# A convolution-attention kernel: six-block slots replaced by eight-block batches, with PSUM and the exponentials as rings

## The chip, the cores and the metric

The kernel runs on one core of a Trainium2 chip. The metric is the device time of one execution in microseconds (us); the time before is the median of three runs. The trace was taken in one further execution by the hardware profiler, and its own time is given beside its span below.

Five engines matter. TensorE (PE in the profile; PEld is its loading of weights) multiplies matrices into PSUM, which has eight banks of 512 float32 a partition. ScalarE (ACT) does the exponentials and most copies out of PSUM, VectorE (DVE) the convolution and most of the elementwise work. GpSimd (POOL) and SyncE (SP) issue transfers for the most part.

## The reference

The input has 4 images of 384 channels and 48 x 48 pixels, so 2304 tokens an image. There are 8 heads of 48 channels.

```python
x_flat = x.reshape(B, C, N).transpose(0, 2, 1)
local = lax.conv_general_dilated(x, conv_w, (1, 1), 'SAME', feature_group_count=C)   # 7 x 7, depthwise
local = local * inv[None, :, None, None] + (bn_beta - bn_mean * inv)[None, :, None, None]
local_flat = local.reshape(B, C, N).transpose(0, 2, 1)
x_norm = _layernorm(x_flat, ln_gamma, ln_beta)
qkv = x_norm @ qkv_w.T + qkv_b
q, k, v = ...                                              # (B, heads, tokens, 48) each
q = q + _layernorm(local_flat, ln_gamma, ln_beta) by heads
attn = softmax(einsum('bhnd,bhmd->bhnm', q, k) * 48 ** -0.5)
out = einsum('bhnm,bhmd->bhnd', attn, v) by tokens @ proj_w.T + proj_b
return (x_flat + out) as an image
```

## The kernel before, in words

**Tiling.** Everything is float32. The queries of an image are cut into five groups of whole rows: 8, 10, 10, 10 and 10 rows of 48 pixels, so 384 columns in the first group and 480 in the others ("narrow" and "wide" in the prediction). Over four images that is 20 groups, t = 0 to 19; t // 5 is the image and t % 5 the group in it. The keys of an image are cut into 18 blocks of 128 tokens, and the 8 heads into 4 pairs (p). A group therefore has 4 x 18 = 72 pieces of work ("blocks"), one for each head pair and key block.

**One block.** `score` (line 1143) makes the scores of 128 keys against the group's queries for both heads of a pair: three passes (the queries and keys are split into a high and a low part, tile `qs` and tile `ks`), each a pair of matmuls, one on each 64-row half of TensorE, so six matmuls into a tile `r` of two PSUM banks, one bank a head. ScalarE then writes the exponentials of both banks in one instruction of 960 (or 768) columns to a tile `pt` in SBUF (line 1151). `weigh` (line 1158) multiplies values by those exponentials: one pair of matmuls, one for each head, each writing one 64-row half of a PSUM bank `o`. In the trace and in the order below a matmul is shown in parts where the hardware counts it in parts: a block has 6 score instructions and 4 value instructions there, or 3 and 2 pairs. The value products of the blocks add up in PSUM. The softmax's denominators come out of the same product, from a column of ones beside the values.

**The slot.** A group runs in `NSLOT` = 12 slots of `BATCH` = 6 blocks, three slots to a head pair. A slot first issues all six scores with their exponentials (`score_batch`), then all six value products (`weigh_batch`), and then `sums_out`: ScalarE copies the sums of the slot from PSUM, at the first slot of a head pair straight to the output tile `ao` or `aot` (line 1045), else to a tile `part_o` (line 1035, named `o` in the profile), which VectorE adds to the output tile in the next slot (`sums_add`, line 1054). PSUM is a pool of four tiles of two banks, taken in turn by scores, sums and everything else (`two_banks`). The exponentials have four buffers.

**What runs beside it.** TensorE, VectorE, ScalarE and SyncE execute their instructions in the order in which the program is written; nothing is reordered. Beside the attention of a group the other engines prepare the next one:

- VectorE computes the 7 x 7 convolution of the next group's rows, one tap of one third of the channels at a time (line 367, tile `acc`). How many taps stand at which place is planned when the program is built: `spare` says for each half of each slot how much of VectorE's time is free, `due` when the taps of each group must be done, and `plan` spreads them. `convolve` issues the planned number. The first taps of a group are ScalarE's (line 330, queued through `soon`).
- The sums are normalized over the 384 channels (`Norm`). In the first image (t = 0 to 3, "early" in the code) the mean is made by TensorE (line 616), kept in SBUF by ScalarE (line 609), subtracted by VectorE, squared by ScalarE (`square_jobs`, line 588), and the root is three activations: logarithm, exponential, square (`root`, lines 652 to 654). VectorE then refines the root (`newton`, from line 666), scales the sums and adds the query projection (line 992, tile `xn`). In the later images the means go through DRAM, so that few elements are left for the root.
- A group's queries are split for each head pair: the high part is a ScalarE cast (`high_queries`, line 1006), the low part a VectorE subtraction (`low_queries`, line 1011), followed by six small transfers that fill the rest of the 128 partitions (lines 1016 and 1018), half of them on SyncE and half on another queue.
- Keys lie in DRAM (`wide`), and stacks of six blocks are loaded by GpSimd's queue two slots before they are needed (`load_keys`, line 801).
- Between two images the projections of the next image run for 140 us on TensorE (line 729). The change does not touch their matmuls.

The order of all this is written out by hand in the loop over slots at the end of the program: after the scores of a slot comes a list of conditions on the slot number, then the first half's taps (`convolve("slot", t, s, 0)`), `sums_add`, more conditions, the value products (with the queued `jobs`, the squares, ahead of them), the second half's taps, and again a list of conditions.

## Time and profile before

| | before |
|---|---|
| median of three runs | 2724.02 us (2722.55 to 2724.08) |
| span of the profiled execution | 2720.3 us |
| TensorE busy | 2707.9 us, 100% of the span |
| VectorE busy | 2314.8 us, 85% |
| ScalarE busy | 1671.1 us, 61% |
| GpSimd busy | 592.7 us, 22% |
| mean granted TensorE clock | 1.000 |
| DMA | 370.46 MB, mean 136 GB/s |

The profiled execution is one execution, of which the profile gives the span, 2720.3 us from the first to the last instruction; its time as the three runs are timed is not recorded apart. The span lies 3.7 us under the median.

How to read the rows of the prediction: in a group of instructions stand line, engine, operation, output and inputs with their shapes and the count, then the busy time in us, the mean time of one in ns, and the idle time of the engine just before these instructions with what ended most of it. In the timeline stand the start in us from the span's beginning, the length in us of a run of like instructions, the engine and what they are with their count (x36), and in brackets, where the engine waited before it, how long and for whom. A timeline cut to a window shows of a run only the instructions that start in the window, so the same run appears with smaller counts, and the difference of two starts divided by the difference of the counts gives the pace. Two matmuls on the two halves of TensorE make a pair. In the row that begins with 246.90:357.40, these are the ends of the stretch; then come its length, the busy us and count of TensorE, its weight loads, VectorE, ScalarE and GpSimd, the granted clock, and the DMA's busy share and GB/s.

### The profile page before, as it was taken

The numbers are of one execution on the slowest core, as the hardware profiler recorded it, in microseconds if no ns is written. First come the engines' busy times: TensorE is split into PE (matmuls) and PEld (weight loads), VectorE is DVE, ScalarE is ACT, GpSimd is POOL, SyncE is SP. The second block draws the span as 40 slices with busy tenths as digits, with TensorE's granted clock in tenths as the row PEclk, the third lists the DMA queues.
The fourth block names the chain that finished last, engine by engine and source line by source line (L and its number), as shares of the span: only waits on it lengthen the run. The fifth ranks groups of instructions, "written<-read, shape, count | busy, mean of one in ns | idle before, by whom it ended". The sixth has DMA issues, their size and how long they took to land.

```text
span 2720.3 us, 46072 instructions
## 1 busy us (share of the span) xinstructions
PE 2707.9 (100%) x16468; PEld 1532.5 (56%) x16468; DVE 2314.8 (85%) x4042; ACT 1671.1 (61%) x2318; POOL 592.7 (22%) x1061
## 2 busy tenths in 40 slices
PE   9999999999999999999999999999999999999999
PEld 6565555555566555555555655555555665555555
DVE  8999999989899999989889999889889898986212
ACT  4366767777326777777622767767752377676762
POOL 3541111112452111011165111111225501110110
PEclk9999999999999999999999999999999999999999
DMA  8454544545455545455455554544635544444442
GB/s 176 91 160 124 140 125 127 134 129 160 129 139 164 145 118 142 124 143 138 122 152 144 154 146 120 139 132 129 167 96 160 151 141 123 147 128 132 139 151 68
DMA packets 160129, 370.46 MB, mean 136 GB/s; under 512 B 58273, under 2 KB 107234, under 8 KB 159890
## 3 DMA queue, kind: packets, MB, share of 16 engines
q0 software_dynamic: 70688, 277.77, 36.0%
q1 hardware_dynamic: 83456, 79.29, 12.9%
q10 hardware_dynamic: 5746, 10.36, 1.1%
q8 instruction: 132, 2.16, 0.3%
q14 instruction: 107, 0.88, 0.1%
HBM read 258.14 MB, written 64.14 MB: 118 GB/s over the span
## 4 chain that ended last, share of the span: by engine, by line
PE 93%; DVE 5%; DMA 1%; ACT 0%; issue 0%; SPq 0%; DVEq 0%; ACTq 0%
PE o L1158 41%; PE r L1143 33%; PE r L729 18%; DVE acc L367 4%; DMA xn<-in_x_dram 1%; DMA staged<-in_qkv_wT_dram 0%; PE r L616 0%; DVE k L839 0%; DMA slab<-in_x_dram 0%; DVE sq L593 0%; DVE ao L1054 0%; SPq L116 0%; PE r L634 0%; DVE xn L644 0%; DVE sq L594 0%
## 5 line engine op out<-in xcount | busy, mean ns | idle before, releaser
L367 DVE SCALAR_TENSOR_TENSOR acc<-slab,vec,acc 128x470 f32<-128x470 f32 (+10 forms) x2832 | 1656.9, 656 | 2.0 <-ACT acc L330 2.0
L1151 ACT ACTIVATE pt<-r 128x960 f32<-128x960 f32 (+1 forms) x1440 | 1248.4, 943 | 244.1 <-PE o L1158 150.4
L1158 PE MATMUL o<-pt,v 128*64 128x480 f32 (+1 forms) x5760 | 1166.1, 554 | 0.4 <-ACT pt L1151 0.4
L1143 PE MATMUL r<-qs,ks 64*128 64x480 f32 (+1 forms) x8640 | 965.8, 373 | 1.6 <-ACT xn L853 0.7
L1143 PEld LDWEIGHTS r<-qs,ks 64*128 64x128 f32 x8640 | 783.6, 184 | 265.6 <-issue 168.2
L1158 PEld LDWEIGHTS o<-pt,v 128*64 128x64 f32 x5760 | 392.9, 137 | 659.2 <-issue 566.8
L801 POOL DMA_DIRECT2D ks<-wide x220 | 159.9, 727 | 1375.7 <-PE r L1143 1333.1
L729 PE MATMUL r<-xn,w_qk 128*128 128x384 f32 x864 | 284.2, 486 | 0.0
L1035 ACT COPY o<-o 113x480 f32<-113x480 f32 (+1 forms) x160 | 87.0, 544 | 275.6 <-PE o L1158 275.4
L729 PEld LDWEIGHTS r<-xn,w_qk 128*128 128x128 f32 x864 | 164.0, 190 | 114.7 <-issue 0.7
L823 ACT COPY v<-r 128x384 f32<-128x384 f32 x72 | 32.0, 480 | 190.3 <-PE r L729 190.3
L729 PE MATMUL r<-w_v,xn 128*128 128x384 f32 x432 | 145.0, 488 | 0.9 <-ACT sq L654 0.5
L1054 DVE TENSOR_TENSOR ao<-ao,o 113x480 f32<-113x480 f32 (+1 forms) x120 | 75.8, 631 | 75.2 <-ACT o L1035 75.2
L729 PEld LDWEIGHTS r<-w_v,xn 128*128 128x128 f32 x432 | 81.4, 190 | 59.9 <-issue 2.9
L786 POOL DMA_DIRECT2D wide<-k x144 | 71.7, 500 | 115.5 <-ACT k L836 79.4
L1011 DVE TENSOR_TENSOR qs<-xn,qs 128x480 fp32r<-128x480 f32 (+1 forms) x60 | 38.0, 633 | 59.1 <-ACT qs L1006 59.1
L729 PE MATMUL r<-af,w_o 128*128 128x384 f32 (+1 forms) x270 | 85.2, 470 | 0.0
L1045 ACT COPY ao<-o 113x480 f32<-113x480 f32 (+1 forms) x60 | 32.6, 544 | 74.3 <-PE o L1158 74.3
L1054 DVE TENSOR_TENSOR aot<-aot,o 113x480 f32<-113x480 f32 (+1 forms) x40 | 25.2, 631 | 58.5 <-ACT o L1035 58.5
L853 ACT ACTIVATE xn<-r,qkb 128x384 f32<-128x384 f32 x72 | 40.2, 577 | 55.1 <-PE r L729 53.8
L1124 DVE SCALAR_TENSOR_TENSOR xr<-r,pb,xr 128x384 f32<-128x384 f32 (+2 forms) x72 | 42.0, 611 | 36.8 <-PE r L729 28.1
L729 PEld LDWEIGHTS r<-af,w_o 128*128 128x128 f32 x270 | 51.3, 190 | 31.9
(154 smaller groups left out, 1338.8 us busy)
## 6 DMA issues: line engine op xcount, KB each, us to landing
ks<-wide POOLq DMA_DIRECT2D x220, 768.0 KB, 5.1
qs<-qs SPq DMA_DIRECT2D x346, 60.0 KB
slab<-in_x_dram POOLq DMA_DIRECT2D x22, 432.0 KB, 6.4
wide<-k POOLq DMA_DIRECT2D x96, 96.0 KB, 2.2
wide<-ks POOLq DMA_DIRECT2D x12, 768.0 KB, 5.1
xr<-in_x_dram POOLq DMA_DIRECT2D x16, 576.0 KB, 5.4
rb<-rden SPq DMA_DIRECT2D x32, 270.0 KB
held<-ao POOLq DMA_DIRECT2D x12, 720.0 KB, 4.1
```

Of the source, the lines that this page charges most:

```text
L367: nc.vector.scalar_tensor_tensor(dst, src, weight, dst, ALU.mult, ALU.add)
L729: nc.tensor.matmul(dst, lhsT=weights(c), rhs=src(c), start=c == 0, stop=c == CC - 1)
L786: nc.gpsimd.dma_start(out=last[16 * u : 16 * u + 16, 0], in_=k[r : r + 16, 0])
L801: queue.dma_start(out=place_keys(b, p, i), in_=wide[b, p][:, :, at])
L853: nc.scalar.activation(src[:, i, :], q[:, :G], AF.Identity, bias=qkb[:, 0, i : i + 1])
L1011: nc.vector.tensor_sub(qs[:, 1, :], query_of(t, p), qs[:, 0, :])
L1035: nc.scalar.copy(part[0 : 64 + HA], sums[0 : 64 + HA, 0, :n])
L1054: nc.vector.tensor_add(dst, dst, part[0 : 64 + HA])
L1124: nc.vector.scalar_tensor_tensor(xr[:, co, :], m, pb[:, co : co + 1], xr[:, co, :], ALU.add, ALU.add)
L1143: nc.tensor.matmul(r[:, j, :n], lhsT=ks[rows, w, at], rhs=qs[rows, m, :], start=i == 0, stop=i == 2,)
L1151: nc.scalar.activation(pt, r[:, :, :n], AF.Exp, scale=SCALE)
L1158: nc.tensor.matmul(sums[halves[j], 0, : columns_of(t)], lhsT=values[t // NA, kb // NB][:, first : first + 64], rhs=pt[:, j, :], start=i == ...
```

## The change

**Batches.** A group runs in 9 batches of 8 blocks instead of 12 slots of 6 (`BATCH`, `NBATCH`). 18 blocks of a head pair are not a multiple of 8, so some batches hold the end of one pair and the start of the next (in a group counted from 1: batches 3, 5 and 7); such a batch uses both banks of its sums' tile, one for each pair, and copies the first out inside the value products and the second behind them. Instead of 4 copies straight to the output and 8 partial sums there are 4 and 8 again (12 sums a group), and `part_o` has one buffer instead of two.

**Rings.** PSUM is one tile of eight banks, and `two_banks` deals out the next two of them in turn; before, a pool of four two-bank tiles did. The exponentials lie in one tile `pt` of nine halves (`2 * SPLIT + 1`, a half being 480 columns), taken in turn, two a block. As nine is odd, one block in nine has its two halves at the two ends of the tile; its exponential is two instructions of half the width (line 1167) instead of one (line 1171).

**Order in a batch.** The scores of all eight blocks are issued one after the other. The exponentials of blocks 1 to 4 and the first half of block 5's are issued with their scores. The second half of 5 and those of 6, 7 and 8 are queued (`exps`) and issued one each behind the value products of blocks 1, 2, 3 and 4, whose halves of the tile they take. In the prediction 5a and 5b are the two halves of the fifth.

**The steps beside it.** The conditions on the slot number are replaced by a table of steps (`steps_of`): each batch has four places, 0 in the middle of the scores (ahead of block 5), 1 behind them, 2 in the middle of the value products (behind block 4), 3 behind them. The convolution's taps are planned for these quarters (`spare`), with `AHEAD`, the point from which the next group's sums begin, at 24 instead of 18. The queued `jobs` are issued behind the first value product and the exponential that follows it, and the three activations of the root in groups t = 1 to 3 are one such job now. Keys are loaded by `next_keys`, as many stacks ahead as before.

The core of the diff, without the planner's numbers and the table's entries that keep their order:

```diff
-BATCH = 6
-NSLOT = 12
+BATCH = 8
+THIRD = 6
+SPLIT = 4
...
-AHEAD = 18
+AHEAD = 24
...
-    ps = ctx.enter_context(tc.tile_pool(name="ps", bufs=4, space=bass.MemoryType.PSUM))
+    ps = ctx.enter_context(tc.tile_pool(name="ps", bufs=1, space=bass.MemoryType.PSUM))
...
-    def two_banks(name="r"):
-        return ps.tile([P, 2, 512], F32, tag="r", name=name)
+    banks = ps.tile([P, 8, 512], F32, tag="banks", name="banks")
+    weights_of = big.tile([P, 2 * SPLIT + 1, GM], F32, tag="pt", name="pt")
+    n_banks = n_weights = 0
+
+    def two_banks():
+        nonlocal n_banks
+        i = n_banks % 8
+        n_banks += 2
+        return banks[:, i : i + 2, :]
...
-        pt = work.tile([P, 2, GM], F32, tag="pt", name="pt", bufs=4)[:, :, :n]
-        nc.scalar.activation(pt, r[:, :, :n], AF.Exp, scale=SCALE)
-        weighing.append((t, p, kb, pt))
...
+        n_halves = 2 * SPLIT + 1
+        first, second = n_weights % n_halves, (n_weights + 1) % n_halves
+        n_weights += 2
+        weighing.append((t, p, kb, (first, second)))
+
+        def exp_of(i, j):
+            nc.scalar.activation(weights_of[:, i, :n], r[:, j, :n], AF.Exp, scale=SCALE)
+
+        def exp_of_both():
+            if second:
+                nc.scalar.activation(
+                    weights_of[:, first : second + 1, :n], r[:, :, :n], AF.Exp, scale=SCALE
+                )
+            else:
+                exp_of(first, 0)
+                exp_of(second, 1)
+
+        if i < SPLIT:
+            exp_of_both()
+        elif i == SPLIT:
+            exp_of(first, 0)
+            exps.append(lambda: exp_of(second, 1))
+        else:
+            exps.append(exp_of_both)
...
-    def weigh_batch(t, s):
-        p, i = s // (KB // BATCH), s % (KB // BATCH)
-        while jobs:
-            jobs.popleft()()
-        while soon:
-            soon.popleft()()
-        sums = two_banks("o")
-        for n in range(BATCH):
-            weigh(n, sums)
-        ended.append((t, p, i, sums))
-        sums_out()
+    def score_batch(t, s, middle):
+        for i, (p, kb) in enumerate(blocks_of(s)):
+            if i == SPLIT:
+                middle()
+            score(t, p, kb, i)
+        return two_banks()
+
+    def weigh_batch(s, t, sums, middle):
+        blocks = blocks_of(s)
+        for n, (p, kb) in enumerate(blocks):
+            j = p - blocks[0][0]
+            start, stop = kb == 0 or n == 0, kb == KB - 1 or n == BATCH - 1
+            weigh(sums[:, j, :], start, stop)
+            if exps:
+                exps.popleft()()
+            if n == 0:
+                while jobs:
+                    jobs.popleft()()
+            if stop:
+                first = p * KB // BATCH
+                ended.append((t, p, s - first, kb == KB - 1, sums[:, j, :]))
+            if n == SPLIT - 1:
+                while soon:
+                    soon.popleft()()
+                middle()
+            if stop:
+                sums_out()
...
+            at(first, 3, lambda: norm.mean_of_sum())
+            at(first + 1, 0, lambda: norm.centre(), lambda: jobs.extend(norm.square_jobs()))
+            if t:
+                at(first + 1, 2, lambda: norm.sum_squares())
+                at(first + 1, 3, lambda: norm.mean_of_sum())
+                at(first + 2, 0, lambda: jobs.extend(norm.root_jobs()))
+                at(first + 2, 2, early_end)
+                at(first + 3, 0, high)
+                at(first + 3, 1, low)
...
+            sums = score_batch(t, s, lambda: step(0))
+            next_keys(b, g, s)
+            step(1)
+            weigh_batch(s, t, sums, lambda: step(2))
+            step(3)
```

How this moves instructions shows at three places. The first is TensorE at the head of the second group (t = 1, the first wide one), before. `qs_0` are its queries of the first head pair, `ks_0_0` to `ks_0_2` the three key stacks of that pair; a row of x36 is six blocks of scores, one of x12 their value products.

```order
L1143 MATMUL r<-qs_0_2189,ks_0_0_2182 128x480 x36
L1158 MATMUL o<-pt,v 64x480 x12
L1143 MATMUL r<-qs_0_2189,ks_0_1_2274 128x480 x36
L1158 MATMUL o<-pt,v 64x480 x12
L1143 MATMUL r<-qs_0_2189,ks_0_2_2367 128x480 x36
L1158 MATMUL o<-pt,v 64x480 x12
```

The same place in the changed kernel, where `ks_1_0` is a stack of the second head pair:

```order
L1154 MATMUL banks<-qs_0_2018,ks_0_0_1930 128x480 x36
L1154 MATMUL banks<-qs_0_2018,ks_0_1_2047 128x480 x12
L1191 MATMUL banks<-pt,v 64x480 x16
L1154 MATMUL banks<-qs_0_2018,ks_0_1_2047 128x480 x24
L1154 MATMUL banks<-qs_0_2018,ks_0_2_2049 128x480 x24
L1191 MATMUL banks<-pt,v 64x480 x16
L1154 MATMUL banks<-qs_0_2018,ks_0_2_2049 128x480 x12
L1154 MATMUL banks<-qs_1_2167,ks_1_0_2157 128x480 x36
L1191 MATMUL banks<-pt,v 64x480 x16
```

Each run of scores is 48 instructions instead of 36 and each run of value products 16 instead of 12; the third batch goes over from the first head pair to the second.

The second place is ScalarE in the same stretch, before: the exponentials of three slots, the sums' copies and the high part of the next pair's queries.

```order
L1151 ACTIVATE pt<-r 128x960 x6
L1006 CAST qs_1_2357<-xn 128x480
L1045 COPY ao_2398<-o 113x480
L1151 ACTIVATE pt<-r 128x960 x6
L1035 COPY o_0_1_2492<-o 113x480
```

And in the changed kernel:

```order
L1171 ACTIVATE pt<-banks 128x960 x4
L1167 ACTIVATE pt<-banks 128x480
L1010 CAST qs_1_2167<-xn 128x480
L1167 ACTIVATE pt<-banks 128x480
L1171 ACTIVATE pt<-banks 128x960 x3
L1049 COPY ao_2199<-banks 113x480
L1171 ACTIVATE pt<-banks 128x960 x4
L1167 ACTIVATE pt<-banks 128x480 x4
L1171 ACTIVATE pt<-banks 128x960 x2
L1039 COPY o_0_1_2303<-banks 113x480
```

A batch has four whole exponentials, the two halves of the fifth, and three more; in the second batch the sixth exponential is also in two halves, since it falls on the ends of the ring. The cast of the queries stands between the halves of the fifth.

The third place is ScalarE near the end of the same group, where the root of the next queries' norm is. Before (`sq` is the norm's buffer, `qs_0_3287` the next group's queries):

```order
L1151 ACTIVATE pt<-r 128x960 x6
L609 COPY sq<-r 128x480
L652 ACTIVATE sq<-sq,eps 128x480
L653 ACTIVATE sq<-sq 128x480
L654 ACTIVATE sq<-sq 128x480
L1045 COPY aot_2399<-o 113x480
L1151 ACTIVATE pt<-r 128x960 x6
L1006 CAST qs_0_3287<-xn 128x480
```

In the changed kernel:

```order
L615 COPY sq<-banks 128x480
L1171 ACTIVATE pt<-banks 128x960 x2
L1167 ACTIVATE pt<-banks 128x480 x2
L1171 ACTIVATE pt<-banks 128x960
L1167 ACTIVATE pt<-banks 128x480 x2
L658 ACTIVATE sq<-sq,eps 128x480
L659 ACTIVATE sq<-sq 128x480
L660 ACTIVATE sq<-sq 128x480
L1171 ACTIVATE pt<-banks 128x960 x3
L1039 COPY o_3_1_2942<-banks 113x480
L1171 ACTIVATE pt<-banks 128x960 x3
L1167 ACTIVATE pt<-banks 128x480 x2
```

The root stood ahead of a slot's sums' copy, behind all its exponentials; now it stands between the fifth exponential and the last three of a batch. The next group's queries follow in the batch behind it, the last of the group; before, their split stood in the eleventh of the twelve slots.

336 lines of the change are left out of this document (164 added, 172 removed).

## The prediction

> **What bounds the kernel now.** I read the page's totals first, then the share of each engine in the chain that ended last, then the groups of instructions with the shapes kept apart.
>
> ```profile
> PE 2707.9 (100%) x16468; PEld 1532.5 (56%) x16468; DVE 2314.8 (85%) x4042; ACT 1671.1 (61%) x2318; POOL 592.7 (22%) x1061
> ...
> PE 93%; DVE 5%; DMA 1%; ACT 0%; issue 0%; SPq 0%; DVEq 0%; ACTq 0%
> ```
>
> ```profile
> L1158 PE MATMUL o<-pt,v 128*64 128x480 f32 x4608 | 969.7, 570 | 0.0
> L1143 PE MATMUL r<-qs,ks 64*128 64x480 f32 x6912 | 800.0, 381 | 0.0
> ...
> L1158 PE MATMUL o<-pt,v 128*64 128x384 f32 x1152 | 196.4, 490 | 0.4 <-ACT pt L1151 0.4
> L1143 PE MATMUL r<-qs,ks 64*128 64x384 f32 x1728 | 165.8, 340 | 1.6 <-ACT xn L853 0.7 <-DMA qs<-qs 0.5 <-ACT pt L1151 0.4
> ```
>
> TensorE is busy all the time and is 93% of the chain. The last column says that the attention matmuls waited about 2 us in the whole run, so there is no wait to remove. What can still go is the time that TensorE spends between its matmuls. The timeline of TensorE over one slot, and then cuts that begin later inside the same two runs, show it.
>
> ```profile
> 486.15 4.17 PE L1143 MATMUL r<-qs,ks 64*128 64x480 f32 x36
> 490.25 5.05 PE L1158 MATMUL o<-pt,v 128*64 128x480 f32 x24
> 495.23 4.17 PE L1143 MATMUL r<-qs,ks 64*128 64x480 f32 x36
> ...
> 486.69 3.63 PE L1143 MATMUL r<-qs,ks 64*128 64x480 f32 x32
> 489.08 1.24 PE L1143 MATMUL r<-qs,ks 64*128 64x480 f32 x10
> 490.70 4.60 PE L1158 MATMUL o<-pt,v 128*64 128x480 f32 x22
> 493.52 1.78 PE L1158 MATMUL o<-pt,v 128*64 128x480 f32 x8
> ```
>
> Matmuls run in pairs. From x32 to x10 lie 11 score pairs in 2.39 us: 0.217 us a pair. From x22 to x8 lie 7 value pairs in 2.82 us: 0.403 us a pair. At that pace 18 score pairs would take 3.91 us, but the next run starts after 4.10; 12 value pairs would take 4.84, and take 4.98. So a slot pays 0.19 + 0.14 = 0.33 us for changing from scores to values and back, whatever its size.
>
> **The change, part by part.** *Fewer changes of kind.* 240 slots of six blocks become 180 batches of eight: 60 x 0.33 = 19.8 us less. Nothing hides this time, since TensorE is the bound, and matmuls are neither added nor dropped.
>
> *The eighth block waits for the fourth exponential.* The ring holds four score pairs, so block 8 of a batch takes the banks of block 4, and its exponential must be over. Six-block slots never needed that: their last block needed the second one. The timeline of ScalarE in the same slot, and both engines in a slot of 384 columns:
>
> ```profile
> 486.27 0.56 ACT L1035 COPY o<-o 113x480 f32<-113x480 f32 x1 [2.13 <-PE o L1158]
> 487.17 3.56 ACT L1151 ACTIVATE pt<-r 128x960 f32<-128x960 f32 x4 [0.34 <-PE r L1143]
> 491.38 0.97 ACT L1151 ACTIVATE pt<-r 128x960 f32<-128x960 f32 x1 [0.66 <-PE o L1158]
> ```
>
> ```profile
> 182.25 3.43 PE L1143 MATMUL r<-qs,ks 64*128 64x384 f32 x36
> 182.71 2.97 PE L1143 MATMUL r<-qs,ks 64*128 64x384 f32 x32
> 183.94 1.74 PE L1143 MATMUL r<-qs,ks 64*128 64x384 f32 x18
> ...
> 183.14 2.92 ACT L1151 ACTIVATE pt<-r 128x768 f32<-128x768 f32 x4 [0.30 <-PE r L1143]
> ```
>
> At 480 columns the fourth exponential ends at 490.73, 4.58 us after the scores began. Unhindered, block 8 (pair 22) would start 0.54 + 19 x 0.217 = 4.66 us after. What a late release costs, one slot with a wait shows: TensorE, its weight loads, and ScalarE.
>
> ```profile
> 636.13 1.24 PE L1143 MATMUL r<-qs,ks 64*128 64x480 f32 x8
> 636.44 0.92 PE L1143 MATMUL r<-qs,ks 64*128 64x480 f32 x6
> 636.77 0.60 PE L1143 MATMUL r<-qs,ks 64*128 64x480 f32 x4
> ...
> 636.44 0.52 PEld L1143 LDWEIGHTS r<-qs,ks 64*128 64x128 f32 x6 [0.34 <-ACT pt L1151]
> ...
> 635.42 0.97 ACT L1151 ACTIVATE pt<-r 128x960 f32<-128x960 f32 x1
> ```
>
> The exponential ended at 636.39 and the waiting weight load began at 636.44, 0.05 later. The matmul began with it, but the pair after it came 0.33 us later instead of 0.217: 0.11 more, since the weights had not been loaded ahead. A release therefore costs nothing only if it comes 0.16 us ahead of the pair's turn. Here 4.58 + 0.16 = 4.74 against 4.66: 0.08 us a batch. At 384 columns the fourth exponential ends at 186.06, 3.81 us in; 9 pairs at (183.94 - 182.71) / 7 = 0.176 us would lead on to 0.46 + 19 x 0.176 = 3.80 us for block 8; 3.81 + 0.16 - 3.80 = 0.17 us a batch.
>
> *Split exponentials.* The ring of nine halves makes one exponential in nine, and the fifth of every batch, two instructions of half the width. In batches 6 to 9 of each group (counting from 1) the split falls on one of the first four exponentials, ahead of block 8. No half-width exponential is in the trace. The nearest rows are a copy out of PSUM of 480 columns with the exponential that follows it (the first of the row under it), and three squares of 480 columns from SBUF.
>
> ```profile
> 634.11 0.54 ACT L1035 COPY o<-o 113x480 f32<-113x480 f32 x1
> 634.55 2.69 ACT L1151 ACTIVATE pt<-r 128x960 f32<-128x960 f32 x3
> ...
> 327.29 1.59 ACT L588 ACTIVATE sq<-acc 128x480 f32<-128x480 f32 x3
> ```
>
> From copy to exponential is 0.44 us, so two halves take 0.88. A full exponential takes (489.74 - 487.17) / 3 = 0.857, by the start of the fourth:
>
> ```profile
> 489.74 0.99 ACT L1151 ACTIVATE pt<-r 128x960 f32<-128x960 f32 x1
> ```
>
> Extra: 0.02 us. The squares lie about 0.50 apart (three in 1.59, of which the last shows 0.6): two of those would cost 0.13 to 0.14 more than one full exponential. I take 0.04, near the copy, since an exponential reads PSUM as the copy does, and keep 0.02 and 0.13.
>
> Of the 180 batches 144 are wide and 36 narrow, and 4 in 9 have the split: 80 x 0.08 + 64 x 0.12 + 20 x 0.17 + 16 x 0.21 = 6.4 + 7.7 + 3.4 + 3.4 = 20.9 us more.
>
> [...]
>
> *Exponentials behind the value products.* Exponentials 5b to 8 are each queued behind the value product that frees their halves. The row at 491.38 shows such a release 1.13 us after the value run's start (490.25); one product is 0.806 us and one exponential 0.857, so number 8 starts near 3.7 us and ends near 4.7, while its own product is due at 0.05 + 7 x 0.806 = 5.7. Cover 1 us: cost nothing. The sums' copy, 0.56 us, still stands ahead of exponential 1, which waits for TensorE (0.34 in the row above).
>
> *Steps at other places.* In groups 2 to 4 of the first image the squares and the root of the next queries' norm are now queued between exponentials 5b and 6, one batch each. The root, and what VectorE and SyncE do behind it:
>
> ```profile
> 337.75 0.69 ACT L652 ACTIVATE sq<-sq,eps 128x480 f32<-128x480 f32 x1
> ...
> 339.11 0.60 ACT L654 ACTIVATE sq<-sq 128x480 f32<-128x480 f32 x1
> ...
> 339.75 0.72 DVE L666 SCALAR_TENSOR_TENSOR sq<-sq,eps 128x480 f32<-128x480 f32 x1 [4.60 <-ACT sq L654]
> ...
> 342.89 1.98 DVE L992 SCALAR_TENSOR_TENSOR xn<-acc,vec,xn 128x480 f32<-128x480 f32 x3
> ...
> 347.55 0.51 SPq L1016 DMA_DIRECT2D qs<-qs  x1
> ...
> 350.01 1.22 SPq L1018 DMA_DIRECT2D qs<-qs  x2
> ```
>
> The root takes 1.96 us (337.75 to 339.71). Exponential 5b starts 1.13 us into the value run and takes 0.44, so exponential 6 ends near 1.6 + 1.9 + 1.0 = 4.5, and its product was due at 0.05 + 5 x 0.806 = 4.1: about 0.5 us, and 0.1 for the squares (1.5 us instead of 1.9) and as much for the query's copy that now stands ahead of exponential 5a. That is 0.7 us a group, 2 us in all. The next group's queries now come in the last batch instead of two slots ahead: VectorE needs 5.1 us behind the root (339.75 to 344.87), then comes to nine taps and an add, and SyncE issues six transfers in 3.7 us (347.55 to 351.23). From the root's end, 9 us into batch 8, that is 9 + 5.1 + 7 + 3.7 = 25 us, and the next group starts after two batches, 24 us. Where all six stand on SyncE (behind groups 2 and 3) I put 0.5 us each, 1 us in all, between 0 and 5. So this part costs 3 us, bounds 0 and 8.
>
> VectorE's taps keep their number; its load is the windows' row of group 2 of the first image:
>
> ```profile
> 246.90:357.40 110.50, 110.50 (x730) 59.71 (x728) 105.44 (x172) 79.46 (x99) 13.78 (x21) 1.00 0.48 131
> ```
>
> 105.4 of 110.5 us: still less than what TensorE will need there (110.5 less 12 - 9 = 3 changes at 0.33, 109.5), so cost nothing, with 4 us of cover. Key loads move to GpSimd's queue in groups by blocks, still 12 blocks ahead (12 x 0.65 us and a value run of 6.6, 14 us) of a need that takes 5 us: nothing.
>
> ```profile
> ks<-wide POOLq DMA_DIRECT2D x220, 768.0 KB, 5.1
> ```
>
> The sum: -19.8 + 20.9 + 3 = +4.1 us. The profiled execution's span is 2720.3 us, 3.7 under the median of the three times, 2724.0, and no other time of it is shown; the same terms added to the median give **2728 us**.
>
> **The rivals.** *Faster: the release need not come early.* If a weight load behind the waiting one is fetched ahead, only real lateness counts: arrival 4.58 + 0.05 = 4.63 is ahead of 4.66 in wide batches, 0.01 late with the split, 0.06 and 0.10 late in narrow ones: 64 x 0.01 + 20 x 0.06 + 16 x 0.10 = 3.4 us instead of 20.9, and 2724.0 - 19.8 + 3.4 + 3 = 2710.6 us. The rows at 636.44 speak against it, where the loss stood on top of the lateness; for it, that slot was late by more than its pair's turn, while here the release comes 0.03 ahead of it. Chance 0.20.
>
> [...] The trace has the loads ahead in steady running and not behind a wait.
>
> *Slower: half-width exponentials cost like the squares.* Place: batches 6 to 9 of each group, before block 8. At 0.13 extra the split batches lose 0.21 and 0.30: 6.4 + 13.4 + 3.4 + 4.8 = 28.0, and 2724.0 - 19.8 + 28.0 + 3 = 2735 us. It decides from an extra of 0.06 us, where the sum passes +0.2%. The copies, which read PSUM as an exponential does, speak against it; the squares, activations of that width, for it. Chance 0.24.
>
> *Slower: VectorE's lag reaches the next group's queries.* Place: the heads of groups 2 to 5 of the first image, where the queries have no time to spare. VectorE ran late there: an add of a partial sum, queued behind half a slot's taps, and that slot's start.
>
> ```profile
> 393.70 0.65 DVE L1054 TENSOR_TENSOR ao<-ao,o 113x480 f32<-113x480 f32 x1
> ...
> 384.70 4.17 PE L1143 MATMUL r<-qs,ks 64*128 64x480 f32 x36
> ```
>
> It starts 9.0 us into the slot, where half of it, 4.5, would be in step: a lag of 4.5 us. If 3 us of it stand at the root, four heads wait 3 us each: 2728 + 12 = 2740 us. It decides from a lag of half a microsecond. For it: the 105.4 us of 110.5. Against it: VectorE waited 4.60 us for the root in that row, so it had caught up. Chance 0.15.
>
> **How the numbers follow.** A measurement of this kernel tells about 0.2% (5.4 us) from no change. The forecast, chance 0.41, lies within; the first rival, 0.20, is faster; the two others, 0.39, are slower. The range runs from 2709, just under the faster rival, to 2742, past both slower rivals. Outside lie both slower rivals at once, 2735 + 12 = 2747 us, and the faster one without the 3 us of the moved steps, 2707.6; for these I leave 2 in 10.
>
> **What would show it.** Right: 180 value runs; slots of about 12.0 us at 480 columns; in most score runs a weight load of block 8 that waits for ScalarE; exponentials of half width about 0.45 us apart; TensorE's group time hardly under 109 us. Wrong: score runs of 48 matmuls in 5.40 us (18 + 6 pairs at pace) without that wait, which is the faster rival; halves 0.50 apart; the first matmul of a group waiting for the transfers of its queries.

## The result, and the profile after

The changed kernel takes 2744.61 us, median of four runs (2741.25 to 2747.34), against 2723.45 us before (2722.55 to 2724.08): 1.0077 times as long, 95% interval 1.0063 to 1.0092. It is slower by 21 us, 2.6 us past the end of the range that was given. Its runs lie 6 us apart where those of the kernel before lie 1.5 apart, and the profiled execution, with a span of 2745.3 us, is the longest of the four. So what the two profiles show adds up to 25.0 us, 4 more than the medians.

First the page of the changed kernel, its totals and the chain that ended last:

```profile
PE 2726.0 (99%) x16468; PEld 1535.6 (56%) x16468; DVE 2315.0 (84%) x4042; ACT 1695.4 (62%) x2598; POOL 593.3 (22%) x1061
...
PE 85%; DVE 9%; DMA 4%; SPq 1%; ACT 1%; issue 0%; POOL 0%; DVEq 0%; ACTq 0%
```

TensorE is 85% of the chain instead of 93%, and VectorE, DMA and SyncE's queue have taken the rest: for some 8% more of the time something else than TensorE's pace is what ends last. Where that is, a table of groups shows. A group lasts from its first score matmul to that of the next, the last one of an image to the end of its value products (groups counted from 1, times from the timelines, us):

| groups | before | changed | difference |
|---|---|---|---|
| 1 (narrow, first image) | 95.5 | 96.4 | +0.9 |
| 2 | 110.5 | 117.4 | +6.8 |
| 3 and 4 | 221.1 | 224.2 | +3.1 |
| 5 | 109.2 | 109.4 | +0.2 |
| 6, 11, 16 (narrow) | 265.8 | 268.7 | +2.9 |
| 7, 8, 9 | 326.7 | 336.3 | +9.5 |
| 10 | 108.9 | 108.9 | 0.0 |
| 12 to 15, 17 to 20 | 871.3 | 871.9 | +0.5 |
| start and end of the program | | | +1.0 |

The row of groups 12 to 15 and 17 to 20 is the batch as such: eight wide groups in which nothing else happens take 109.0 us instead of 108.9. The timeline of the second batch of group 14 shows why, TensorE's matmuls and weight loads and ScalarE:

```profile
1832.76 5.56 PE L1154 MATMUL banks<-qs,ks 64*128 64x480 f32 x48
1833.78 3.56 ACT L1171 ACTIVATE pt<-banks 128x960 f32<-128x960 f32 x4 [0.34 <-PE banks L1154]
1837.39 0.52 PEld L1154 LDWEIGHTS banks<-qs,ks 64*128 64x128 f32 x6 [0.23 <-ACT pt L1171]
1838.24 6.66 PE L1191 MATMUL banks<-pt,v 128*64 128x480 f32 x32
```

The scores take 1838.24 - 1832.76 = 5.48 us where 24 pairs at pace with one change of kind would take 5.40, and the last block's weight load waits for ScalarE, as the prediction had it. The value products take 6.6.

The head of group 2 is the largest single loss. TensorE and GpSimd's queue, and the clock in stretches of a microsecond:

```profile
246.60 0.76 POOL L804 DMA_DIRECT2D ks<-wide  x1
247.36 0.51 POOL L1022 DMA_DIRECT2D qs<-qs  x1
248.29 0.98 PE L1154 MATMUL banks<-qs,ks 64*128 64x480 f32 x4 [0.17 <-DMA qs<-qs]
252.31 7.74 PE L1154 MATMUL banks<-qs,ks 64*128 64x480 f32 x44 [3.05 <-DMA qs<-qs]
```

```profile
250.00:251.00 1.00, 0.00 (x0) 0.00 (x0) 1.00 (x2) 0.00 (x0) 0.00 (x0) 1.00 0.97 384
251.00:252.00 1.00, 0.00 (x0) 0.00 (x0) 1.00 (x3) 0.00 (x0) 0.00 (x0) 0.51 0.28 87
...
257.00:258.00 1.00, 1.00 (x9) 0.96 (x8) 1.00 (x3) 0.91 (x2) 0.00 (x0) 0.58 0.20 46
```

The last transfer of the group's queries stands on GpSimd's queue behind a load of keys. TensorE waits 3.05 us for it, the granted clock falls to half, and stays there for 6.8 us, to 257.84. The first run of scores takes 11.7 us instead of 5.5: half of the loss of 6.2 is waiting (0.17 + 3.05), half the clock. VectorE was not late there: it stood waiting 5.73 us for the root of these queries. Groups 3 and 4 wait 0.3 to 0.4 us at a time for the same transfers, and their first runs take 6.2 and 6.6 us.

In the same groups the root of the next norm holds up one batch each. ScalarE and TensorE in the eighth batch of group 2:

```profile
346.40 7.14 PE L1191 MATMUL banks<-pt,v 128*64 128x480 f32 x32
...
349.79 2.68 ACT L1171 ACTIVATE pt<-banks 128x960 f32<-128x960 f32 x3
352.51 0.20 PEld L1191 LDWEIGHTS banks<-pt,v 128*64 128x64 f32 x4 [0.67 <-ACT pt L1171]
```

The next run of scores starts at 353.47, so this run takes 353.47 - 346.40 = 7.07 us instead of 6.59; groups 3 and 4 have the same.

Groups 7 to 9 the prediction had not looked at. The timeline of ScalarE and TensorE in group 8:

```profile
1107.57 4.24 PE L1191 MATMUL banks<-pt,v 128*64 128x480 f32 x18
...
1110.90 0.21 ACT L713 ACTIVATE few_u<-few 128x12 f32<-128x12 f32 x1 [3.78 <-DVE few L708]
...
1112.12 3.61 PE L1191 MATMUL banks<-pt,v 128*64 128x480 f32 x14 [0.30 <-ACT pt L1167]
```

Three small activations (the root of a norm in the later images, `few_root`) stand ahead of exponentials 5b to 8 now, and wait 3.78 us for VectorE, which is late. The value run takes 8.08 us. What VectorE itself waits for, its list of waits says; first the kernel before, then the changed one (us in total, times, longest):

```profile
DVE rd L1080 <- DMA rd<-den: 25.8, 7, 6.3
DVE few L691 <- DMA four<-parts: 24.0, 16, 4.6
```

```profile
DVE rd L1084 <- DMA rd<-den: 66.6, 15, 10.4
DVE few L694 <- DMA four<-parts: 50.4, 22, 5.7
```

VectorE waits 67 us more for transfers in the whole run. The same two rows for groups 7 to 9 alone, before and changed:

```profile
DVE rd L1080 <- DMA rd<-den: 9.3, 2, 5.5
DVE few L691 <- DMA four<-parts: 2.5, 1, 2.5
```

```profile
DVE rd L1084 <- DMA rd<-den: 13.5, 3, 4.9
DVE few L694 <- DMA four<-parts: 10.9, 3, 5.7
```

The waits are twice as long there, and VectorE, busy for 94 and 96% of groups 7 and 8 before, has little time to spare. Most of what is new is the second row, the sums of a norm. The first row is the load of the softmax's denominators ahead of their reciprocal (`divide`): the kernel before had two such waits in these groups too, and TensorE lost nothing by them. In the timeline of SyncE's queue and VectorE, group 8 of the changed kernel, one sees it behind the sums of another norm:

```profile
1063.10 0.59 SPq L685 DMA_DIRECT2D four<-parts  x1
1063.74 0.48 SPq L1074 DMA_DIRECT2D rd<-den  x1
...
1069.60 0.34 DVE L1084 RECIPROCAL rd<-rd 128x30 f32<-128x30 f32 x1 [4.88 <-DMA rd<-den]
...
1073.49 0.56 ACT L1039 COPY o<-banks 113x480 f32<-113x480 f32 x1 [1.36 <-DVE ao L1058]
```

The load is issued only behind the norm's transfers. VectorE stands for 4.9 us, and 4 us later ScalarE's copy of the sums waits for VectorE's add, since `part_o` has one buffer. The changed kernel with two buffers was not run.

### The profile page after: what moved, and what is told of

Read it like the earlier page. It is cut to its first block, busy times and chain, and to the rows that moved or that the text cites. A ratio compares the mean times of both kernels' runs of the same rounds, so it can differ in the third digit from the quotient of the medians.

```text
span 2745.3 us, 45834 instructions
## 1 busy us (share of the span) xinstructions
PE 2726.0 (99%) x16468; PEld 1535.6 (56%) x16468; DVE 2315.0 (84%) x4042; ACT 1695.4 (62%) x2598; POOL 593.3 (22%) x1061
## 4 chain that ended last, share of the span: by engine, by line
PE 85%; DVE 9%; DMA 4%; SPq 1%; ACT 1%; issue 0%; POOL 0%; DVEq 0%; ACTq 0%
PE banks L1191 35%; PE banks L1154 30%; PE banks L732 19%; DVE acc L373 6%; DMA parts<-part 1%; DMA qs<-qs 1%; DMA slab<-in_x_dram 0%; DMA four<-parts 0%; DMA staged<-in_qkv_wT_dram 0%; SPq L1022 0%; PE banks L622 0%; DVE xn L996 0%; DVE qs L1015 0%; DMA rd<-den 0%; SPq L394 0%
## 5 line engine op out<-in xcount | busy, mean ns | idle before, releaser
L1191 PE MATMUL banks<-pt,v 128*64 128x480 f32 (+1 forms) x5760 | 1161.6, 554 | 1.9 <-ACT pt L1167 1.4
L1171 ACT ACTIVATE pt<-banks 128x960 f32<-128x960 f32 (+1 forms) x1120 | 978.7, 945 | 125.1 <-PE banks L1154 81.2
L1154 PE MATMUL banks<-qs,ks 64*128 64x480 f32 (+1 forms) x8640 | 979.6, 376 | 6.5 <-DMA qs<-qs 5.7
L1154 PEld LDWEIGHTS banks<-qs,ks 64*128 64x128 f32 x8640 | 785.3, 185 | 261.5 <-issue 135.2
L1191 PEld LDWEIGHTS banks<-pt,v 128*64 128x64 f32 x5760 | 393.9, 137 | 684.0 <-issue 614.2
L1167 ACT ACTIVATE pt<-banks 128x480 f32<-128x480 f32 (+1 forms) x640 | 342.6, 569 | 220.1 <-PE banks L1191 216.2
L732 PE MATMUL banks<-xn,w_qk 128*128 128x384 f32 x864 | 284.2, 486 | 0.0
L732 PEld LDWEIGHTS banks<-xn,w_qk 128*128 128x128 f32 x864 | 164.0, 190 | 114.7 <-issue 0.7
L1039 ACT COPY o<-banks 113x480 f32<-113x480 f32 (+1 forms) x160 | 87.2, 545 | 172.2 <-PE banks L1191 170.8
L732 PE MATMUL banks<-w_v,xn 128*128 128x384 f32 x432 | 145.0, 488 | 1.1 <-DVE xn L727 0.6
L826 ACT COPY v<-banks 128x384 f32<-128x384 f32 x72 | 34.3, 478 | 168.6 <-PE banks L732 168.6
```

What stands on the lines that cost most here:

```text
L732: nc.tensor.matmul(dst, lhsT=weights(c), rhs=src(c), start=c == 0, stop=c == CC - 1)
L1039: nc.scalar.copy(part[0 : 64 + HA], sums[0 : 64 + HA, :n])
L1154: nc.tensor.matmul(r[:, j, :n], lhsT=ks[rows, w, at], rhs=qs[rows, m, :], start=n_th == 0, stop=n_th == 2,)
L1167: nc.scalar.activation(weights_of[:, i, :n], r[:, j, :n], AF.Exp, scale=SCALE)
L1171: nc.scalar.activation(weights_of[:, first : second + 1, :n], r[:, :, :n], AF.Exp, scale=SCALE)
L1191: nc.tensor.matmul(sums[halves[j], :n], lhsT=values[t // NA, kb // NB][:, first : first + 64], rhs=weights_of[:, at[j], :n], start=start, ...
```

## The experiments

All times are medians, ratios are against the kernel before on the same chip. The changed kernel is the base unless another is named.

**Is the eighth block's wait what eats the saving?** Exponentials 1 to 4 leave out the last 48 columns of each half. The ring is cleared once at the start, which puts off the first group by 3.8 us.

```diff
+        m = n - 48 if i < SPLIT else n
-            nc.scalar.activation(weights_of[:, i, :n], r[:, j, :n], AF.Exp, scale=SCALE)
+            nc.scalar.activation(weights_of[:, i, :m], r[:, j, :m], AF.Exp, scale=SCALE)
```

> Exponentials 1 to 4 of each batch leave out the last 48 columns of each half, so the fourth ends 0.32 us earlier. Theory one (block 8 waits for the fourth exponential): score runs fall from 5.49 and 5.55 to 5.40 us at 480 columns (18 and 6 more pairs at pace) and from 4.6 to 4.41 at 384, 144 x 0.12 + 36 x 0.2 = 24 us less, about 2720 us. Rival (a longer run of scores is slower by itself, or the change of kind costs more than 0.33 us): score runs stay at 5.49, 2744 us.

It took 2733.02 us (ratio 1.0034, 1.0021 to 1.0048), 11.6 less, and 15.4 less without the clearing. The second batch of group 14 in its timeline:

```profile
1828.60 5.47 PE L1156 MATMUL banks<-qs,ks 64*128 64x480 f32 x48
1829.62 3.25 ACT L1175 ACTIVATE pt<-banks 128x864 f32<-128x864 f32 x4 [0.34 <-PE banks L1156]
...
1833.99 6.66 PE L1195 MATMUL banks<-pt,v 128*64 128x480 f32 x32
```

From 1828.60 to 1833.99 are 5.39 us: the wait is gone, and the run is back at pace. The eight quiet wide groups take 864.0 us instead of 871.9 (0.98 each), the three narrow ones 1.5 less each; if all 16 and 4 groups fell as these do, that would be 21.8 us. In this profile the groups other than 7 to 9 fell by 16.7 us together, the first image's five by 3.7, and groups 7 to 9 stayed long (337.6 us). So the rest of the loss is another matter.

**The split exponentials.** Every batch takes the nine halves from the first on, so that none but the fifth is split.

```diff
-        first, second = n_weights % n_halves, (n_weights + 1) % n_halves
+        first, second = 2 * i % n_halves, (2 * i + 1) % n_halves
```

> Each batch takes the nine halves from the first on, so only the fifth exponential is split. Theory one (a split among the first four exponentials delays block 8 by a little): the score runs of 5.54 to 5.56 us become 5.49, and 4.65 becomes 4.59: 64 x 0.06 + 16 x 0.06 = 5 us less, about 2740 us. Rival (the split is hidden): no change, 2744 us.

2745.51 us (ratio 1.0082, 1.0068 to 1.0096): no gain in the time. In the profile the quiet wide groups fell from 871.9 to 870.4 us, 0.18 a group or 0.04 for each split among the first four: the size in the sum was right, and it is too small to be seen beside the 6 us by which runs of this kernel differ. ScalarE's own rows in the changed kernel agree: two halves start 0.451 us apart and two whole exponentials 0.853 (medians, where the second did not wait), so a split costs it 0.05 us.

**The queries at the heads.** Two kernels: in the first the queries of the first image come earlier, in the second only one queue is changed.

```diff
-        return 5 + (t == 0)
+        return 5
-                at(first + 3, 0, high)
-                at(first + 3, 1, low)
+                at(first + 3, 0, high, low)
```

> The first image's next queries come earlier: in the first group the whole chain by one batch, in groups 2 to 4 the low part ahead of the last batch's taps. Theory one (the first matmul of groups 2 to 4 waits for these transfers, and in group 2 the clock falls behind the wait): first score runs of 11.70, 6.24 and 6.62 us come back to 5.5, 8.1 us less, about 2736 us, and the clock stays at 1.00 in group 2. Rival (VectorE is full in the first image, so whoever is late only changes): the waits return at other places of these groups, 2741 to 2747 us.

2739.45 us (ratio 1.0062, 1.0048 to 1.0075), 5.2 less. The head of group 2 in its timeline, and the clock there:

```profile
249.44 5.58 PE L1154 MATMUL banks<-qs,ks 64*128 64x480 f32 x48
```

```profile
249.40:254.90 5.50, 5.50 (x50) 4.34 (x48) 5.50 (x10) 4.90 (x7) 0.72 (x1) 1.00 0.00 0
```

The group took 111.2 us instead of 117.4 and the clock stayed at 1.00, as expected; groups 3 and 4 still took 223.6.

```diff
-            other = nc.sync if 0 < t < NA - 2 else nc.gpsimd
+            other = nc.sync if t < NA - 2 else nc.gpsimd
```

> The changed kernel; only the second half of the first group's next queries goes out on SyncE's queue instead of GpSimd's. Theory (the last transfer stood behind a load of keys on GpSimd's queue): the wait of 3.05 us at the head of the second group falls to 1.5 or less, the clock stays at 1.00, the group takes about 112 us instead of 117.3, and the time 2739 us. Rival (VectorE made the queries too late): the wait stays at 2.5 us or more, with the half clock, 2744 us.

2739.70 us (ratio 1.0057, 1.0043 to 1.0071), 4.9 less. The group took 114.7 us, 2.6 less, so this was right in part. The rest of the 4.9 us is not at this head: in the profile groups 7 to 9 came to 331.9 us instead of 336.3, where this edit changes nothing.

```profile
248.96 0.45 PE L1154 MATMUL banks<-qs,ks 64*128 64x480 f32 x1 [0.45 <-DMA qs<-qs]
250.39 0.70 PE L1154 MATMUL banks<-qs,ks 64*128 64x480 f32 x4 [0.98 <-DMA qs<-qs]
251.49 1.00 PE L1154 MATMUL banks<-qs,ks 64*128 64x480 f32 x4 [0.40 <-DMA qs<-qs]
```

```profile
251.00:252.00 1.00, 0.60 (x6) 0.52 (x6) 1.00 (x2) 0.00 (x0) 0.00 (x0) 0.86 0.00 0
252.00:253.00 1.00, 1.00 (x8) 0.98 (x6) 1.00 (x3) 0.87 (x1) 0.00 (x0) 0.50 0.00 0
...
255.00:256.00 1.00, 1.00 (x12) 0.97 (x11) 1.00 (x3) 0.95 (x2) 0.00 (x0) 0.94 0.20 48
```

Without the key load ahead of it the waits add up to 1.8 us, not 3.2, and the half clock lasts 3.4 us, not 6.8. It did not stay at 1.00 as expected. So the queue was 1.4 us of the wait, and the rest is that the queries come in the group's last batch. Whether the queue also made half of the slow stretch is open: in the kernel with the halves taken anew the key load still stands ahead, TensorE waits 3.32 us, and the half clock lasts 3.4 us as well (253.52 to 256.93).

**Groups 7 to 9.** Three kernels. In the first the small roots stand behind the last exponential (place 2 instead of 1).

```diff
-            at(5, 1, lambda: norm_x.few_root())
+            at(5, 2, lambda: norm_x.few_root())
-            at(6, 1, lambda: norm.few_root())
+            at(6, 2, lambda: norm.few_root())
```

> The three small activations of the norms' root in groups 7 to 9 stand behind the last exponential of their batch instead of ahead of exponential 5b. Theory one (they wait there for VectorE and hold up exponentials 5b to 8, and so the value products): value runs of 7.2 to 8.2 us in these groups come back to 6.6, 5.4 us less in all, about 2739 us. Rival (VectorE's lag is the cause, and the wait only moves to the next batch's head): score runs there grow by as much, 2744 us.

2744.96 us (ratio 1.0081, 1.0067 to 1.0095): no gain. Its profile shows ScalarE's waits for VectorE there cut; the changed kernel first, then this one:

```profile
ACT few_u L713 <- DVE few L708: 21.7, 10, 3.9
```

```profile
ACT few_u L713 <- DVE few L708: 8.7, 6, 2.3
```

Groups 7 to 9 took 330.3 us in it instead of 336.3. But these groups vary: in the four kernels above, which leave their steps as they are, they took 331.9 to 337.6 us. And that execution was the shortest of its five, 3.7 us under the median, as the changed kernel's was the longest of four. What the other four lost again isn't known; their granted clock was 0.997 or 0.998. The time shows no gain by this step alone.

In the second kernel the division as a whole is one step later:

```diff
-            at(1, 3, begin)
+            at(2, 1, begin)
```

> The changed kernel with the softmax's division (load of the denominators, reciprocal, and what follows) issued behind the scores of the third batch instead of behind the values of the second. Theory two (VectorE waits there for the denominators' transfer, 66.6 us in 15 groups against 25.8 in 7 before the change, and this lag is what holds ScalarE and then TensorE in groups 7 to 9): these waits fall under 25 us, the three groups from 336.3 us together to 329, so about 2737 us. Rival (their loss is only the small roots' place): waits fall, the time does not, 2744 us.

2752.75 us (ratio 1.0104, 1.0089 to 1.0120), slower by 8. VectorE's waits for the denominators fell from 66.6 to 2.8 us, and groups 7 and 8 from 224.6 to 218.1. Group 9 stayed at 112.4 without any such wait; VectorE waited 6.5 us for a norm's sums in it, and the small roots 7.1 us for VectorE. And group 14 went from 108.9 to 118.3:

```profile
1868.97 0.46 PE L1154 MATMUL banks<-qs,ks 64*128 64x480 f32 x1 [0.66 <-DMA qs<-qs]
1872.01 1.17 PE L1154 MATMUL banks<-qs,ks 64*128 64x480 f32 x4 [2.58 <-DMA qs<-qs]
1875.40 4.33 PE L1154 MATMUL banks<-qs,ks 64*128 64x480 f32 x19 [2.23 <-DMA qs<-qs]
```

On SyncE's queue the division's transfers now stand ahead of those of the third pair's queries, and TensorE waited 5.5 us for them, with the granted clock at 0.50 from 1871.0 to 1881.2 us. In the third kernel only the load moves, ahead of the norm's transfers, and the reciprocal stays:

```diff
+            def load():
+                loaded[t] = sums_in(t - 1)
+
+            at(1, 1, load)
             def begin():
-                ratios[t] = divide(t - 1)
+                ratios[t] = divide(t - 1, loaded.pop(t))
```

> The changed kernel with one thing different: the denominators are loaded behind the scores of the second batch, the reciprocal stays behind its values. Theory two (VectorE's 66.6 us of waiting there make the lag of groups 7 to 9): the waits fall under 15 us, groups 7 and 8 come to 109 to 110 us each, group 14 stays at 108.9, 4 to 6 us less in all, about 2739 us. Rival (only the small roots' place counts): waits fall, groups 7 to 9 stay at 336 us, 2744 us.

2738.64 us (ratio 1.0057, 1.0043 to 1.0071), 6.0 less. The timeline in group 8, and VectorE's waits:

```profile
1057.01 0.59 SPq L1074 DMA_DIRECT2D rd<-den  x1
...
1061.92 0.33 DVE L1084 RECIPROCAL rd<-rd 128x30 f32<-128x30 f32 x1
```

```profile
DVE rd L1084 <- DMA rd<-den: 43.1, 14, 15.6
```

Here the reciprocal doesn't wait. Groups 7, 8 and 9 took 110.2, 108.9 and 108.8 us, and group 14 stayed at 108.9. The waits did not fall under 15 us as expected: 43.1 are left, 17.8 of them in the last group and behind it, where VectorE has little to do; in groups 7 to 9 they fell from 13.5 to 5.7, and those for the norms' sums from 10.9 to 4.5. The three groups came to 327.9 us, under the 331.9 to 337.6 of the profiles that leave them alone, so the place of this load is worth 4 to 10 us there by the profiles. The small roots are where they were, and wait 6.1 us in all, against 11.5 to 26.1 in those profiles: they were held by VectorE's lateness, and the place of this load made a good part of it. Which of the two kinds of wait made VectorE late isn't told apart, since the one edit cut both.

**Together, in eight-block batches.** Queries earlier, small roots later and the halves anew, by the edits shown above:

> Eight-block batches with the queries earlier, the small roots later, and nine halves taken anew in each batch. Theory one (the changed kernel's loss against the one before is the moved steps; the eighth block's wait only takes back what the fewer changes of kind give): from the 2739.5 us of the kernel with earlier queries, 4.1 us of value runs over 6.6 and 5.3 go, and 16 x 0.12 us of splits: 2733 us. Rival (VectorE's load in the first image and in groups 7 to 9 is the bound there): 2738 us or more, and groups of 111 us and over.

2736.05 us (ratio 1.0044, 1.0030 to 1.0058). Groups 7 to 9 still took 331.6 us in it, group 10 was long (110.8), and so were groups 3 and 4 (223.3). The same with the division later:

> Eight-block batches with all the moved steps mended: queries earlier, small roots later, halves taken anew, division later. Theory two: groups 7 to 10, 342.4 us together in the kernel without the last of these, go to 330 + 109 = 437 minus 108.9 for one, that is 329 for groups 7 to 9 and 108.8 for group 10; about 5 us under that kernel's 2736.1 us, 2731 us. Rival (VectorE is late there for other reasons): 2736 us.

2739.16 us (ratio 1.0055, 1.0041 to 1.0069): groups 7 to 9 came to 330.2 us, and group 14, as above, to 116.3. It did not reach the 2731 us that was expected. Two more with the chain of the later images' norms spread over more batches, and the division in the fourth batch (first) or its load early (second):

```diff
-            at(4, 2, lambda: norm.squares())
-            at(4, 3, lambda: norm.sum_squares(), lambda: norm.out())
+            at(5, 0, lambda: jobs.extend(norm.square_jobs()))
+            at(5, 3, lambda: norm.sum_squares(), lambda: norm.out())
...
-            at(7, 2, lambda: high_queries(t + 1, 0))
-            at(7, 3, lambda: low_queries(t + 1, 0))
+            at(8, 0, lambda: high_queries(t + 1, 0))
+            at(8, 1, lambda: low_queries(t + 1, 0))
...
-            at(1, 3, begin)
+            at(3, 0, begin)
```

> Nine batches of eight with the chain of the following norms relaxed (squares one batch later, centring and roots later, division behind the transfers of the queries) and the queries of the first image earlier. Theory (the batches themselves are neutral, all loss is in the moved steps): groups 6 to 10 come to 89.3 and 108.8 each, 8 us less than in the kernel with earlier queries and later roots, 2728 us, what is left being the heads of the first image and the narrow groups. Rival (eight-block batches leave VectorE or the queues too little time, whatever the order): 2735 us or more.

> Nine batches of eight, queries of the first image earlier, the following norms' chain relaxed, halves taken anew, and the denominators loaded behind the scores of the second batch, half a batch ahead of the reciprocal. Theory (the batches are neutral, the loss is in waits that the steps bring): VectorE's waits for the denominators under 15 us, groups 6 to 15 at 89.3 and 108.8 us, about 2728 us. Rival (eight-block batches leave too little time to the steps in any order): 2735 us or more.

2831.94 us (ratio 1.0398, 1.0384 to 1.0412) and 2756.23 us (1.0124, 1.0109 to 1.0140). Both miss, by waits that my own order brought: in the first VectorE waited 168.8 us for the denominators, whose load stood behind the queries' transfers; in the second the next queries had slipped into the last batch, and heads waited. VectorE's waits for the denominators were 34.3 us there, not under 15.

```profile
DVE rd L1084 <- DMA rd<-den: 168.8, 17, 17.2
```

```profile
PE banks L1153 <- DMA qs<-qs: 9.4, 11, 1.9
```

In the second one, groups 7 to 10 took 109.2 to 109.5 us each, of which 0.5 at the head: the batches themselves are at 12.08 us there too.

**Other sizes in the same structure.** Twelve batches of six, and ten of seven or eight (eight of 7, two of 8), with the steps at matching places and the squares and roots behind the last exponential:

```diff
-BATCH = 8
+SIZES = 7, 7, 7, 7, 8, 7, 7, 7, 7, 8
...
-        return [divmod(i, KB) for i in range(s * BATCH, (s + 1) * BATCH)]
+        return [divmod(i, KB) for i in range(FIRST_OF[s], FIRST_OF[s + 1])]
...
-            if n == 0:
+            if n == SPLIT - 1:
                 while jobs:
```

> The changed kernel's rings, halves and table of steps, but twelve batches of six blocks, with the steps at the places of the kernel before and the squares and roots behind the last exponential. Theory one (rings and split exponentials cost nothing by themselves, only the eighth block's wait and the moved steps do): wide groups of 108.9 us, as in the kernel before, 2723 to 2726 us. Rival (the rings, or more instructions on ScalarE, cost time themselves): groups over 109.5 us, 2735 us or more.

> Ten batches, eight of seven blocks and two of eight, in the same structure, with a batch to spare for the next queries. Theory one (only the eighth block of a batch waits): a batch of seven takes 21 x 0.217 + 0.19 + 14 x 0.403 + 0.14 = 10.53 us, one of eight 12.08, so a wide group 108.4 and a narrow one 88.2: 16 x 0.5 + 4 x 0.3 = 9 us under the kernel before, 2714 us, and up to 2718 with waits left at the heads of the first image. Rival (the seventh block waits as the eighth did): wide groups of 108.9 or more, 2723 us or over.

2784.16 us (ratio 1.0225, 1.0211 to 1.0239) and 2739.65 us (1.0060, 1.0046 to 1.0074). The quiet groups are as expected, 108.9 us in the one and 108.4 in the other. The loss is at other places, in the kernel of six:

```profile
PE banks L1156 <- ACT o_True L1042: 22.7, 9, 8.8
```

```profile
DVE rd L1087 <- DMA rd<-den: 116.2, 17, 14.8
```

The sums' copy (named `o_True` here) waits for VectorE's add and holds TensorE. With the division one step later and the means' centring half a batch later, both again:

```diff
-            at(1, 3, begin)
+            at(2, 1, begin)
-            at(4, 0, lambda: norm.few_centre())
+            at(4, 2, lambda: norm.few_centre())
```

> Batches of six in the changed structure with the division and the centring later. Theory two: the waits of VectorE for the denominators fall from 116 to under 40 us, TensorE's 22.7 us of waiting for the sums' copies goes, and 2784 us come to about 2735. Rival (taps planned wrongly, or another wait): 2770 us or more.

> Batches of seven and eight with the division and the means' centring later. Theory two (VectorE's waits for transfers make it late; the copy of the sums then waits for the single buffer of the partial sums): groups 8 and 9 come from 115.4 and 116.2 us to 108.5 each and group 7 from 110.0 to 108.5, 16 us less, 2724 us or a little under. Rival (too many taps are planned for these groups, whatever VectorE waits for): 2735 us or more.

2760.01 us (ratio 1.0128, 1.0113 to 1.0144) and 2723.13 us (1.0000, 0.9991 to 1.0009). The kernel of six did not reach the 2735 us that was expected: VectorE's waits for the denominators fell to 25.8 us and TensorE's for the sums' copies to 5.9, but TensorE now waited 13.2 us for queries and 12.5 for keys. The kernel with batches of seven gets 16.5 us back; groups 8 and 9 took 108.4 and 108.5 us in its profile, which is the shortest of its eleven executions. Two of its batches in group 18:

```profile
2352.19 4.82 PE L1156 MATMUL banks<-qs,ks 64*128 64x480 f32 x42
2356.94 5.86 PE L1192 MATMUL banks<-pt,v 128*64 128x480 f32 x28
2362.72 4.83 PE L1156 MATMUL banks<-qs,ks 64*128 64x480 f32 x42
```

A batch takes 2362.72 - 2352.19 = 10.53 us, what was worked out from the pace, and no weight load of the scores waits. The same kernel with the division behind the queries' transfers, `at(3, 0, begin)`:

> Batches of seven and eight with the division behind the transfers of the third pair's queries. Theory (what was left in that kernel were transfers of queries behind the division's): groups at 108.45, narrow ones at 88.8, the first image as before: 2715 to 2719 us, under the kernel before. Rival (something else varies there): 2723 us as with the division earlier.

2787.09 us (ratio 1.0232, 1.0218 to 1.0246). Against the 2.9 us of the kernel with 2723.13 us, VectorE now waited

```profile
DVE rd L1087 <- DMA rd<-den: 152.8, 17, 15.5
```

```profile
PE banks L1156 <- ACT o_True L1042: 24.6, 17, 7.5
```

So 64 us hang on the place of the division and its load. And with that load early instead, `at(1, 1, load)` and `at(2, 1, begin)`:

> Batches of seven and eight with the division in the third batch and its load in the second. Theory: wide groups 108.45, narrow ones 88.8, as in the best profile of the kernel with the division later, without its waits for queries: 2715 to 2719 us, under the kernel before. Rival (a few microseconds vary there for another reason): 2723 us.

2723.34 us (ratio 0.9997, 0.9988 to 1.0006), the same as with the division later. No version tried beats the kernel before: batches of seven save 0.5 us in each of eleven wide groups, and give it back in the narrow groups, the first image and at single groups (7 and 14 in one profile, 7, 9 and 10 in the other).

**One buffer for the partial sums, in the kernel before:**

```diff
-            part = work.tile([P, GM], F32, tag="part_o", name=f"o{t}_{p}_{i}")[:, :n]
+            part = work.tile([P, GM], F32, tag="part_o", name=f"o{t}_{p}_{i}", bufs=1)[:, :n]
```

> The kernel before, with one buffer instead of two for the partial sums. Theory (with one buffer ScalarE's copy of a slot's sums waits for VectorE's add of the slot before, wherever VectorE is late): that add ended 9.65 us into its slot where VectorE was 4.5 us late, the copy is due at 9.2, so 0.5 us in such slots, 1 to 4 us in all, 2724 to 2727 us. Rival (VectorE is never that late for long): 2723 us, no change.

2724.57 us (ratio 1.0006, 0.9997 to 1.0015). ScalarE waited there for VectorE's adds,

```profile
ACT o L1035 <- DVE ao L1054: 11.0, 4, 4.4
```

but this cost TensorE 1.5 us, in group 7. A single buffer is harmless as long as VectorE isn't late.

## Why the prediction was wrong

*Fewer changes of kind and the eighth block's wait* (-19.8 and +20.9 us): right. Eight wide groups without other trouble came to 109.0 us against 108.9, batches of 12.08 us, block 8's weight load waiting, a score run of 5.48 us that falls to 5.39 when the fourth exponential ends earlier. With that wait taken away the quiet wide groups fall by 0.98 us and the narrow ones by 1.5, 21.8 us if all groups did. The saving of the change is there, and this is where it goes. The narrow groups' part was right as well, 0.9 to 1.1 us each more (9 x 0.17 + 4 x 0.04 - 3 x 0.33 = 0.7 in the sum).

*The faster rival* (a late release need not cost): refuted by the same rows. That a load behind the waiting one is fetched ahead was the rival's assumption, and no run shows it: in the second batch of group 14 block 8's first pair came at 1837.41, in its turn (1832.76 + 4.66 = 1837.42), and 0.08 to 0.09 us were lost all the same (5.48 us against 5.40 at pace and 5.39 without the wait). *Half-width exponentials*: 0.04 us extra a split by the quiet groups, as in the forecast, and 0.05 by ScalarE's rows, not the 0.13 of the second rival.

*Steps at other places* (3 us, bounds 0 and 8): this step failed. It had two parts. The root in groups 2 to 4 was right, 0.48 us a group against 0.5. The queries at the heads were put at 0.5 us each in two groups, the third and fourth, whose first runs lost 0.7 and 1.1. The head of group 2, whose six transfers go out on two queues, was in no term, and lost 6.2; groups 2 to 5 lost 10.2 us in the profile, 1.4 of them by the root. The key loads on GpSimd's queue were put at nothing because the keys themselves come in time; that a query transfer would stand behind one was not asked, and it made the wait there 1.4 us longer. The half clock behind a wait was in no term either, though at the head of group 2 it is as large as the wait (3.0 us of the 6.2 beside 3.2). The third rival had these heads, at 3 us each in four groups, with chance 0.15, but for another reason, VectorE's lag, and at the worst of them VectorE was ahead, waiting 5.73 us for the root. Its sign, a group's first matmul waiting for its queries, came true without its cause.

The other part was missing altogether. The prediction went through the moved steps of the first image and left out those of the later images, of which there are more: a load of the denominators that VectorE uses at once, now behind a norm's transfers, and three small activations that wait for VectorE, now ahead of four exponentials. Groups 7 to 9, where these stand, lost 9.5 us in the profile, which is the longest of the four executions. The experiment with the load alone moved shows that its place costs about 6 us by the times. It does not show that the wait for the denominators as such does: that wait grew by 4.2 us in these groups, the one for the norms' sums by 8.4, and the load's place changed both. Whether the small roots' place costs anything by itself stays open: moving it alone changed the profile and not the median. Also "cost nothing" for VectorE rested on its busy time, 105.4 of 110.5 us in group 2; over the run the busy time stayed (2314.8 and 2315.0 us), and its waits for transfers grew by 67 us.

With the load early or the queries early the kernel takes 2739 us, with the queries, the small roots and the halves mended together 2736. The two edits that gained most, the load and the queries early, were not run together without other changes, so whether their gains add up is open. That an eight-block kernel reaches the 2728 us of the forecast was not shown: each of the orders tried brought a wait of its own. Shown is that the batches in it take what the sum had.

## What to carry to other kernels

When a change rewrites the order of the steps beside the bound engine, list every step in every kind of stage, not only where the bound engine stood before, and ask of each that waits (an activation on another engine's result, a load used at once) what is queued behind it on its engine and on its DMA queue. A saving per change of kind is worth what is left after the ring's first late release: the batch just short of that wait (seven here) keeps it, the next longer one gives it back. VectorE, busy for 94 and 96% of groups 7 and 8 before, had little room for waits on transfers: in groups 7 to 9 11.8 us of them cost TensorE nothing, and 24.4 us went with a loss of 9.5. So issue such a load a step ahead of its use, which alone took 6.0 us off the changed kernel.

## What the runs showed of the hardware

The granted clock of TensorE fell to half at waits of a few microseconds and less. In the changed kernel it fell at 251.02 us, inside the wait of 3.05 us (249.26 to 252.31) at the head of group 2, and stayed there for 6.8 us, to 257.84. With one queue changed it fell behind waits of 0.45, 0.98 and 0.40 us and stayed for 3.4 us (251.72 to 255.12); with the halves taken anew, where TensorE waited 3.32 us, for 3.4 us as well (253.52 to 256.93). In the kernel with the division later it was at half for 10.2 us (1871.0 to 1881.2), at waits of 0.66, 2.58 and 2.23 us. It stayed at 1.00 in the changed kernel behind the waits of 0.29 and 0.38 us at the heads of groups 3 and 4. In the 3.4 us ahead of the fall TensorE was busy for 1.5 us in the first of these cases and for 1.6 in the second. What sets the length of such a stretch was not shown.

A weight load that waited for its bank cost time though its block was not late. In the second batch of group 14 block 8's load waited 0.23 us for ScalarE and began at 1837.39. The block's first pair of matmuls came at 1837.41, 0.22 us behind the pair ahead of it and so at pace; the second came at 1837.72, 0.31 us later instead of 0.217. Over the 144 wide score runs the medians are 0.219 us ahead of that first pair and 0.304 behind it. In group 14 the score run took 5.48 us, and 5.39 in the kernel whose exponentials end earlier, where no load waited.
